# A spectral convolution block and a selective-scan block on one core: the first projection in two halves side by side, first transfers in order of need, the 64-channel block first, pieces of x asked for earlier

## The chip, the cores and the metric

The kernel runs on one core of a Trainium2 chip, in one launch. The metric is the device time of that core in microseconds (us). A core has five engines that run their own instruction streams in order and wait for each other by semaphores: PE (TensorE, matrix products into PSUM), DVE (VectorE), ACT (ScalarE), POOL (GpSimd) and SP (SyncE, which issues every DMA of this kernel). Sixteen DMA engines carry out the transfers.

## The reference

Two layers over x of 16 images, 64 x 64 pixels, 96 channels, each with a group normalisation before it and a residual sum. The first upsamples by 2 in frequency, applies a quadratic activation between two linear maps, and filters down again. The second is a Mamba-like block with four scan directions:

```python
def _L0_conv_ref(x, W1, b1, W2, b2, coef):
    xu = _upsample_rfft(xc)
    h = h @ W1.T + b1
    h = coef[:, 0] + coef[:, 1] * h + coef[:, 2] * (h * h)
    h = h @ W2.T + b2
    hl = _lpf_rfft(hc, cutoff=0.5)
    out = hl[:, :, ::2, ::2]
...
def _L1_conv_ref(x):
    xz = jnp.einsum('bhwc,pc->bhwp', x, in_proj_w)
    xc, z = (xz[..., :d], xz[..., d:])              # d = 192
    z = silu(z)
    xc = silu(depthwise_3x3(xc) + conv_b)
    xs = jnp.stack([x0, x1, x0[..., ::-1], x1[..., ::-1]], axis=1)   # rows, columns, both reversed
    x_dbl = jnp.einsum('bkdl,kcd->bkcl', xs, x_proj_weight)
    dts, Bs, Cs = jnp.split(x_dbl, [R, R + N], axis=2)               # R = 6, N = 16
    dts = jnp.einsum('bkrl,kdr->bkdl', dts, dt_projs_weight)
    # delta = softplus(dts + bias); h = exp(delta * A) * h + delta * u * B; y = sum_n h * C
    ys = selective_scan(xs, dts, As, Bs, Cs, Ds, dt_projs_bias)
    # y: the four directions summed, layer norm, times z
    return jnp.einsum('bhwd,cd->bhwc', y, out_proj_w)
...
x = x + _L0_conv_ref(_gn(x))
x = x + _L1_conv_ref(_gn(x))
```

## The kernel before

The program is written out engine by engine in its final order (`tc.manual_schedule()`); nothing reorders it. Its parts are generators, and a `yield` in them is the end of a slice.

**front(mi)** (L240) makes everything of an image that the scan needs. It normalises the image and goes over 100 rows of the upsampled picture in four passes of 25 (L313). A pass fetches x in three pieces of 32 channels, `fetch_x(cg)` (L264), four DMAs of 128 KB and two buffers each, multiplies them with the upsampling matrix (`u_ps`, L324) and copies the result to `t1` (L335). Then come five groups of five rows: `xu` (widened and normed), `h_ps` (L365), squares `hsq` on ACT (L348), `o_ps` (L377). Each second group is narrowed again and stowed in DRAM (`narrow`, `stow`, L303). Pieces of x, xu, hsq and others share eleven buffers (`piece`, L192). In each pass the first piece is asked for at the pass's start (L316), followed by three empty slices; the next one after the products of the one before (L331).

The second half of front computes the depthwise convolution as nine products with shifted pictures (L482), silu on ACT, and the z branch. It runs over two blocks of channels, `for i, n, tiles, both` (L461): first the 128 channels in eight tiles, then the 64 others in four tiles with two halves of the picture side by side. `turn` (L466) copies each tile into `col`, the column-wise order (L467), and stores rows and z in DRAM (L473, L474). After a block `col` is stored: for the 128 channels as four DMAs of 512 KB (L508, the helper's L199), for the 64 channels as eight DMAs of 128 KB in runs of 32 elements, 128 bytes (L513). `col` has one buffer, tag b16; the convolution's picture `xgp` and t1 have one other, tag b18.

**project(mi, pair, lc, out)** (L633) makes delta, delta * u, B and C of one step: a stretch of T = 1024 positions, in two halves of TB = 512 one after the other (L651). For a half it loads u in three parts (L645), multiplies them with the projection (`pp`, L655), adds the bias (`pr`, L659), and for each third of the channels, in the order 0, 2, 1: `s` (L666); softplus on ACT by way of |s|, exp, relu, ln (e, m, w, d: L674 to L681); four products with the identity that add up w, e, d, m (L686); dtu on DVE (L691), delta copied on ACT (L692); both stored in DRAM (L695, L696). B and C go to `rows` (L669). Every tile of it has one buffer.

**scan()** (L615) runs 128 steps (16 images, two pairs of directions, four stretches) of 24 units, 3072 in all. A unit covers 128 rows of (channel, state) twice: `drive` b = dtu * B on POOL (L761); `decay` exp(delta * A) on ACT (L755); the recurrence on DVE (L770, L772); the product with C on POOL (L917), DVE (L927), or DVE at every fifth unit (L909); the read-out on PE (L794). b, c, dtu and delta are loaded from DRAM with repetition (L703, L722). Decay runs one unit ahead, drive two.

Beside the units runs the background. Three times in a unit `slot` (L852) takes a slice of the next step's projection and one of the next image's front; when front is through, of the last image's finish. `Background` (L822) paces them: SLICES = 550 weights of front and finish over POS = 576 slots of an image.

Before the scan nothing runs beside anything: front of image 0, the whole first projection (L738), then the loads of eight b and c, of dtu and of delta (L740 to L742), then `drive` for two units and `decay` for one (L866 to L869). After it comes finish of the last image.

Of the kernel before, what the change touches and what calls it, by code (L numbers as in the profile page):

```python
# [45 lines left out]
F32 = mybir.dt.float32  # L46
# [25 lines left out]
SLICES = 550  # L72
# [7 lines left out]
def tile_two_blocks(  # L80
# [159 lines left out]
    def front(mi):  # L240
# [71 lines left out]
        o_last = None  # L312
        for p0 in range(0, UPS, PP):  # L313

            t1 = b18.tile([HW, PP, C], F32, name="t1", tag="b18")
            xr = fetch_x(0)  # L316
            for _ in range(3):
                yield
            for cg in range(3):
                u_ps = [bank([HW, 16, PP], "u_ps") for _ in range(2)]  # L320
                for k in range(16):
                    for a in range(2):
                        on = slice(64 * a, 64 * a + 64)
                        nc.tensor.matmul(  # L324
                            u_ps[a][:, k, :], lhsT=xr[k // 8][on, k % 8, :], rhs=up_s[on, p0:p0 + PP],
                            start=True, stop=True,
                        )
# [13 lines left out]
            for g in range(PP // PG):  # L341
# [119 lines left out]
        for i, n, tiles, both in ((0, 128, 8, 0), (1, 64, 4, 4)):  # L461
# [153 lines left out]
    def scan():  # L615


        with ExitStack() as es:
# [9 lines left out]
            banks.append(es.enter_context(tc.tile_pool(name="b_ps", bufs=2, space=PSUM)))  # L628
            aps = es.enter_context(tc.tile_pool(name="sc_aps", bufs=2, space=PSUM))
            yps = es.enter_context(tc.tile_pool(name="sc_yps", bufs=1, space=PSUM))  # L630
            gps = es.enter_context(tc.tile_pool(name="sc_gps", bufs=1, space=PSUM))

            def project(mi, pair, lc, out):  # L633
# [3 lines left out]
                out["rows"] = rows = dctx.tile([2, 2 * NS, T], F32, name="rows")  # L637
                out["delta"] = [dctx.tile([128, T], F32, name=f"delta_d{v}") for v in range(3)]
                out["dtu"] = [dctx.tile([128, T], F32, name=f"dtu_d{v}") for v in range(3)]
                xs_d = image[mi]["xs"]  # L640
                order = (0, 2, 1)

                def fetch_u(v, t):
                    uv = up_.tile([128, TB], F32, name="u")
                    nc.sync.dma_start(out=uv, in_=xs_d[v, :, lc * T + t:lc * T + t + TB])  # L645
                    return uv

                ahead_u = [fetch_u(v, 0) for v in order]
                for _ in range(4):
                    yield  # L650
                for t in range(0, T, TB):  # L651
                    u, ahead_u = dict(zip(order, ahead_u)), []
                    pp = gps.tile([128, TB], F32, name="pp", tag="g")
# [4 lines left out]
                    pr = pj.tile([128, TB], F32, name="pr")  # L658
# [3 lines left out]
                    for i, v in enumerate(order):  # L662
                        if i == 0:
                            yield
                        s = gps.tile([128, TB], F32, name="s", tag="g")
# [7 lines left out]
                        e, d, m, w = (pj.tile([128, TB], F32, name=k) for k in ("e", "d", "m", "w"))  # L673
# [9 lines left out]
                        s = gps.tile([128, TB], F32, name="s", tag="g")  # L683
# [5 lines left out]
                        dtu = pj.tile([128, TB], F32, name="dtu")  # L689
                        delta = pj.tile([128, TB], F32, name="delta")  # L690
# [6 lines left out]
                        if t + TB < T and i < 2:  # L697
# [364 lines left out]
```

## Time and profile before

| | us |
|---|---|
| median of 3 runs | 21647.74 (21629.93 to 21659.27) |
| profiled execution | 21651.91 |
| its span, first to last instruction | 21650.1 |
| first tile of the convolution starts on PE | 320.29 |
| first projection starts on PE | 438.13 |
| first product of the scan on POOL | 538.28 |
| first scan on DVE | 542.99 |
| last image's finish, from | 21497 |

The profiled execution and its span lie 1.8 us apart. In the profile a line such as "538.28 8.95 POOL L761 ..." of a timeline reads: start, duration, engine, line of the kernel, operation, output <- inputs with their shapes, how often, and in brackets how long the engine was idle before it and what ended that. SPq lines are DMA issues on SP. A line of the waits reads: what waited <- for what: us in total, times, longest. The granted TensorE clock was 0.857 in the mean.

### The profile page before, as it was taken

The page shows a single profiled execution, that of the slowest core. Times are in us where ns is not written, and L with a number is a line of the kernel's source. Part 1 is how long each engine was busy: PE and PEld are TensorE (multiplying, and loading weights), DVE is VectorE, ACT ScalarE, POOL GpSimd, SP SyncE. Part 2 cuts the span into 40 slices and gives each one's busy share as a digit, 9 for nine tenths or more (in the row PEclk, how much of TensorE's full clock was granted, in tenths as well). Part 3 has the DMA queues.
Part 4 walks back from the last instruction along what each step waited for, and adds up shares of the span by engine and source line. Part 5 has one row for each costly group of instructions (what it writes and reads, how often), then busy time and mean ns, then how long its engine had stood idle before and what let it go on. Part 6 is the DMA issues. An engine that isn't in the chain of part 4 may idle for free. (4 is left out here: it accounts for less than half of the span.)

```text
span 21650.1 us, 273738 instructions
## 1 busy us (share of the span) xinstructions
PE 16910.3 (78%) x98988; PEld 7341.1 (34%) x98988; DVE 19532.7 (90%) x12983; ACT 13726.8 (63%) x20546; POOL 19514.3 (90%) x5538
## 2 busy tenths in 40 slices
PE   7776877877778787887778788787787778877855
PEld 4423324233342333324333242333423333243221
DVE  0999999999999999999999999999999999999997
ACT  3666666666666666666666666676666666666553
POOL 0999999999999999999999999999999999999996
PEclk8887888988889888888888888888898888988977
DMA  2565565656656566565655656566565665656654
GB/s 71 182 206 183 201 220 185 222 188 204 217 184 224 185 216 200 191 226 180 219 194 201 221 183 215 192 204 213 191 226 182 214 201 193 225 181 219 216 188 141
DMA packets 1855467, 4277.13 MB, mean 198 GB/s; under 512 B 449438, under 2 KB 548670, under 8 KB 1852062
## 3 DMA queue, kind: packets, MB, share of 16 engines
q1 hardware_dynamic: 1854110, 4259.62, 59.0%
q8 instruction: 781, 12.80, 0.3%
q14 instruction: 576, 4.72, 0.1%
HBM read 3380.58 MB, written 878.18 MB: 197 GB/s over the span
## 5 line engine op out<-in xcount | busy, mean ns | idle before, releaser
L761 POOL TENSOR_TENSOR b<-dtu,bt 128x2048 f32<-128x2048 f32 x3072 | 13898.6, 4531 | 1341.2 <-PE y L794 617.3
L755 ACT ACTIVATE da<-delta,a_s 128x1024 f32<-128x1024 f32 x6144 | 6845.6, 1116 | 3099.3 <-DVE b L770 795.3
L917 POOL TENSOR_TENSOR b<-b,ct 128x1024 f32<-128x1024 f32 x2458 | 5798.8, 2359 | 631.1 <-DVE new L778 291.2
L794 PE MATMUL y<-b,fold_s 128*32 128x256 f32 x49152 | 3623.5, 420 | 331.3 <-DVE b L927 141.1
L927 DVE TENSOR_TENSOR b<-da,ct 128x1024 f32<-128x1024 f32 x3072 | 3756.6, 1223 | 93.9
L770 DVE TENSOR_TENSOR_SCAN da<-da,new,b 128x1024 f32<-128x1024 f32 x1383 | 3247.0, 2348 | 386.8 <-ACT da L755 361.7
L772 DVE TENSOR_TENSOR_SCAN da<-da,new,b 128x1024 f32<-128x1024 f32 x1382 | 3242.8, 2346 | 230.3 <-ACT da L755 212.4
L794 PEld LDWEIGHTS y<-b,fold_s 128*32 128x32 f32 x49152 | 1386.6, 117 | 2917.1 <-issue 1271.0
L686 PE MATMUL s<-w,ident_s 128*128 128x512 f32 x1536 | 1212.9, 882 | 1345.3 <-ACT w L681 1265.6
L772 DVE TENSOR_TENSOR_SCAN b<-da,new,b 128x1024 f32<-128x1024 f32 x922 | 2157.9, 2340 | 45.9 <-ACT da L755 36.3
L770 DVE TENSOR_TENSOR_SCAN b<-da,new,b 128x1024 f32<-128x1024 f32 x921 | 2156.3, 2341 | 13.3 <-ACT da L755 8.5
L778 ACT COPY new<-da 128x1 f32<-128x1 f32 x2764 | 434.6, 157 | 2723.5 <-DVE b L927 2195.3
L482 PE MATMUL c_ps<-xgp,wtap_s 96*128 96x512 f32 (+1 forms) x4608 | 1694.3, 635 | 163.2 <-ACT row L500 158.7
L666 PE MATMUL s<-pr,dtw_s 128*128 128x512 f32 x1536 | 1005.9, 741 | 1000.2 <-ACT pr L659 495.9
L365 PE MATMUL h_ps<-xu,w1t_s 96*128 96x500 f32 x1920 | 1044.0, 644 | 293.7 <-ACT hsq L348 120.6
L377 PE MATMUL o_ps<-w2c_s,hsq 128*100 128x96 f32 x9600 | 1061.3, 270 | 187.0 <-ACT hsq L348 161.8
L772 DVE TENSOR_TENSOR_SCAN da<-da,b 128x1024 f32<-128x1024 f32 x461 | 1055.9, 2291 | 120.4 <-ACT da L755 120.0
L770 DVE TENSOR_TENSOR_SCAN da<-da,b 128x1024 f32<-128x1024 f32 x460 | 1053.7, 2291 | 121.0 <-ACT da L755 116.5
L655 PE MATMUL pp<-u,xpt_s 128*128 128x512 f32 x1536 | 922.1, 741 | 305.7 <-DMA u<-xs_d 205.0
L377 PEld LDWEIGHTS o_ps<-w2c_s,hsq 128*100 128x100 f32 x9600 | 992.2, 182 | 393.0 <-ACT hsq L348 218.9
L686 PE MATMUL s<-e,ident_s 128*128 128x512 f32 x1536 | 1088.3, 800 | 0.0
L482 PEld LDWEIGHTS c_ps<-xgp,wtap_s 96*128 96x128 f32 (+1 forms) x4608 | 611.5, 173 | 1113.8 <-issue 896.3
(128 smaller groups left out, 21643.8 us busy)
## 6 DMA issues: line engine op xcount, KB each, us to landing
dtu<-dtu_d SPq DMA_DIRECT2D x1536, 512.0 KB
delta<-delta_d SPq DMA_DIRECT2D x1536, 512.0 KB
bt<-rows SPq DMA_DIRECT2D x1024, 512.0 KB
ct<-rows SPq DMA_DIRECT2D x1024, 512.0 KB
u<-xs_d SPq DMA_DIRECT2D x896, 256.0 KB
dtu_d<-dtu SPq DMA_DIRECT2D x768, 256.0 KB
delta_d<-delta SPq DMA_DIRECT2D x768, 256.0 KB
xr<-in_x SPq DMA_DIRECT2D x768, 128.0 KB
```

Source lines behind the costliest of these rows:

```text
L365: nc.tensor.matmul(h_ps[j], lhsT=w1t_s[:, 128 * j:128 * (j + 1)], rhs=xu.rearrange("c p q -> c (p q)"), start=True, stop=True,)
L377: nc.tensor.matmul(o_ps[:, p, :], lhsT=hsq[j][:, UPS * p:UPS * (p + 1)], rhs=w2c_s[:, j, :], start=(j == 0), stop=(j == HB - 1),)
L482: nc.tensor.matmul(c_ps[p:p + n], lhsT=wtap_s[:, tap, 128 * i:128 * i + n], rhs=xgp[:, h0:h0 + 8, dx:dx + HW], start=(tap == 0), stop=(tap ...
L666: nc.tensor.matmul(s, lhsT=dtw_s[:, pair, v, :], rhs=pr, start=True, stop=True)
L686: nc.tensor.matmul(s, lhsT=ident_s, rhs=of, start=(k == 0), stop=(k == 3))
L755: nc.scalar.activation(da, deltas[n // NQ, e], AF.Exp, scale=a_s[:, k, g, units[n][2]:units[n][2] + 1])
L761: nc.gpsimd.tensor_mul(b, dtus[n // NQ], bt.unsqueeze(1).to_broadcast([128, 2, T]))
L770: nc.vector.tensor_tensor_scan(out, da, b, before, ALU.mult, ALU.add)
L772: nc.vector.tensor_tensor_scan(out[:, ::-1], da[:, ::-1], b[:, ::-1], before, ALU.mult, ALU.add)
L794: nc.tensor.matmul(y[32 * q:32 * q + 32, e, :], lhsT=fold_s, rhs=b[:, e, QT * q:QT * q + QT], start=(pair == 0 and j == 0 and e == 0), sto ...
L917: nc.gpsimd.tensor_mul(h, h, bc[1, r, j])
L927: nc.vector.tensor_mul(bs[n][:, 0, :], h, bc[1, r, j])
```

## The change

Five edits. The first step's projection is started as two generators, one for each half, that take turns slice by slice; the second has buffers of its own, cut out of the b16 and b18 buffers (`far_u`, `far_w`), and both share four PSUM banks (`side_ps`), so the scan's PSUM pools are opened after it. As soon as one third of the channels is stored for both halves, the first b, dtu and delta are asked for; the seven other loads of b and c follow the projection. In front the 64-channel block comes before the 128-channel one. Pieces of x are kept in a list: the first pass asks for two at its start and for the third after the first products; in each pass's last group of rows the first two pieces of the next pass are asked for. The three empty slices thus remain in the first pass only, and SLICES goes from 550 to 541. For all later steps project runs as before, both halves in one generator.

```diff
-SLICES = 550
+SLICES = 541
...
         o_last = None
+        asked = []
         for p0 in range(0, UPS, PP):
 
             t1 = b18.tile([HW, PP, C], F32, name="t1", tag="b18")
-            xr = fetch_x(0)
-            for _ in range(3):
-                yield
+            if not asked:
+                asked += [fetch_x(0), fetch_x(1)]
+                for _ in range(3):
+                    yield
             for cg in range(3):
+                xr = asked.pop(0)
...
-                if cg < 2:
-                    xr = fetch_x(cg + 1)
+                if cg == 0:
+                    asked.append(fetch_x(2))
                 yield
...
                     if j == 2 and sd is not None:
                         stow(sd, row - 2 * PG)
+                    if j >= 2 and g == PP // PG - 1 and p0 + PP < UPS:
+                        asked.append(fetch_x(j - 2))
...
-        for i, n, tiles, both in ((0, 128, 8, 0), (1, 64, 4, 4)):
+        for i, n, tiles, both in ((1, 64, 4, 4), (0, 128, 8, 0)):
...
-            banks.append(es.enter_context(tc.tile_pool(name="b_ps", bufs=2, space=PSUM)))
-            aps = es.enter_context(tc.tile_pool(name="sc_aps", bufs=2, space=PSUM))
-            yps = es.enter_context(tc.tile_pool(name="sc_yps", bufs=1, space=PSUM))
-            gps = es.enter_context(tc.tile_pool(name="sc_gps", bufs=1, space=PSUM))
-
-            def project(mi, pair, lc, out):
+            def project(mi, pair, lc, out, ps, half=None, own=None):
...
+                halves = range(0, T, TB) if half is None else (half,)
+
+                def make(name):
+                    return own(name) if own else pj.tile([128, TB], F32, name=name)
...
-                ahead_u = [fetch_u(v, 0) for v in order]
+                ahead_u = [fetch_u(v, halves[0]) for v in order]
...
-                for t in range(0, T, TB):
+                for t in halves:
...
-                        if t + TB < T and i < 2:
+                        out["made"] += 1
+                        if half is None and t + TB < T and i < 2:
...
-            for _ in project(*steps[0], ctxs[0]):
-                pass
-            bc = {(what, 0, j): fetch_bc(ctxs[0], 0, j, what) for j in range(NQ) for what in range(2)}
-            dtus = {0: fetch_dtu(ctxs[0], 0)}
-            deltas = {(0, e): fetch_delta(ctxs[0], 0, e) for e in (1, 0)}
+
+            bc, dtus, deltas = {}, {}, {}
+
+            far_u = b16.tile([128, 4, TB], F32, name="far_u", tag="b16")
+            far_w = b18.tile([128, 6, TB], F32, name="far_w", tag="b18")
+            far = {f"u{v}": far_u[:, v, :] for v in range(3)}
+            far["pr"] = far_u[:, 3, :]
+            far.update({k: far_w[:, i, :] for i, k in enumerate(("e", "d", "m", "w", "dtu", "delta"))})
+            with tc.tile_pool(name="side_ps", bufs=4, space=PSUM) as side:
+                todo = [project(*steps[0], ctxs[0], side, 0), project(*steps[0], ctxs[0], side, TB, far.get)]
+                while todo:
+                    todo = [g for g in todo if next(g, todo) is not todo]
+                    if ctxs[0]["made"] >= 2 and not dtus:
+                        bc[0, 0, 0] = fetch_bc(ctxs[0], 0, 0, 0)
+                        dtus[0] = fetch_dtu(ctxs[0], 0)
+                        for e in (1, 0):
+                            deltas[0, e] = fetch_delta(ctxs[0], 0, e)
+            for j in range(NQ):
+                for what in range(2):
+                    if (what, 0, j) not in bc:
+                        bc[what, 0, j] = fetch_bc(ctxs[0], 0, j, what)
+            banks.append(es.enter_context(tc.tile_pool(name="b_ps", bufs=2, space=PSUM)))
+            aps = es.enter_context(tc.tile_pool(name="sc_aps", bufs=2, space=PSUM))
+            yps = es.enter_context(tc.tile_pool(name="sc_yps", bufs=1, space=PSUM))
+            gps = es.enter_context(tc.tile_pool(name="sc_gps", bufs=1, space=PSUM))
+
...
-                    step_gen = Background(project(*steps[st], ctxs[st]), PSLICES, 3 * per_step)
+                    step_gen = Background(project(*steps[st], ctxs[st], gps), PSLICES, 3 * per_step)
```

More of the change, by code (lines that the diff above doesn't have):

```diff
@@ L627, in scan @@
             dctx = es.enter_context(tc.tile_pool(name="dctx", bufs=3, space=bass.MemoryType.DRAM))
-            banks.append(es.enter_context(tc.tile_pool(name="b_ps", bufs=2, space=PSUM)))
-            aps = es.enter_context(tc.tile_pool(name="sc_aps", bufs=2, space=PSUM))
-            yps = es.enter_context(tc.tile_pool(name="sc_yps", bufs=1, space=PSUM))
-            gps = es.enter_context(tc.tile_pool(name="sc_gps", bufs=1, space=PSUM))
-            def project(mi, pair, lc, out):
-                out["rows"] = rows = dctx.tile([2, 2 * NS, T], F32, name="rows")
-                out["delta"] = [dctx.tile([128, T], F32, name=f"delta_d{v}") for v in range(3)]
-                out["dtu"] = [dctx.tile([128, T], F32, name=f"dtu_d{v}") for v in range(3)]
+            def project(mi, pair, lc, out, ps, half=None, own=None):
+                if not out:
+                    out["rows"] = dctx.tile([2, 2 * NS, T], F32, name="rows")
+                    out["delta"] = [dctx.tile([128, T], F32, name=f"delta_d{v}") for v in range(3)]
+                    out["dtu"] = [dctx.tile([128, T], F32, name=f"dtu_d{v}") for v in range(3)]
+                    out["made"] = 0
+                rows = out["rows"]
                 xs_d = image[mi]["xs"]
                 order = (0, 2, 1)
+                halves = range(0, T, TB) if half is None else (half,)
+                def make(name):
+                    return own(name) if own else pj.tile([128, TB], F32, name=name)
                 def fetch_u(v, t):
-                    uv = up_.tile([128, TB], F32, name="u")
+                    uv = own(f"u{v}") if own else up_.tile([128, TB], F32, name="u")
                     nc.sync.dma_start(out=uv, in_=xs_d[v, :, lc * T + t:lc * T + t + TB])
                     return uv
-                ahead_u = [fetch_u(v, 0) for v in order]
+                ahead_u = [fetch_u(v, halves[0]) for v in order]
                 for _ in range(4):
                     yield
-                for t in range(0, T, TB):
+                for t in halves:
                     u, ahead_u = dict(zip(order, ahead_u)), []
-                    pp = gps.tile([128, TB], F32, name="pp", tag="g")
+                    pp = ps.tile([128, TB], F32, name="pp", tag="g")
                     for v in range(3):
@@ L657, in project @@
                         yield
-                    pr = pj.tile([128, TB], F32, name="pr")
+                    pr = make("pr")
                     nc.scalar.activation(pr, pp, AF.Identity, bias=bumps_s)
@@ L664, in project @@
                             yield
-                        s = gps.tile([128, TB], F32, name="s", tag="g")
+                        s = ps.tile([128, TB], F32, name="s", tag="g")
                         nc.tensor.matmul(s, lhsT=dtw_s[:, pair, v, :], rhs=pr, start=True, stop=True)
@@ L672, in project @@
                         yield
-                        e, d, m, w = (pj.tile([128, TB], F32, name=k) for k in ("e", "d", "m", "w"))
+                        e, d, m, w = (make(k) for k in ("e", "d", "m", "w"))
                         nc.scalar.activation(e, s, AF.Abs)
@@ L682, in project @@
                         yield
-                        s = gps.tile([128, TB], F32, name="s", tag="g")
+                        s = ps.tile([128, TB], F32, name="s", tag="g")
                         yield
@@ L688, in project @@
                             yield
-                        dtu = pj.tile([128, TB], F32, name="dtu")
-                        delta = pj.tile([128, TB], F32, name="delta")
+                        dtu, delta = make("dtu"), make("delta")
                         nc.vector.tensor_mul(dtu, s, u[v])
```

## The prediction

> **What bounds the kernel now.** I read the page's busy shares first, then POOL's and DVE's timelines, then every engine's timeline from 390 to 546 us, then the waits.
>
> ```profile
> PE 16910.3 (78%) x98988; PEld 7341.1 (34%) x98988; DVE 19532.7 (90%) x12983; ACT 13726.8 (63%) x20546; POOL 19514.3 (90%) x5538
> DVE  0999999999999999999999999999999999999997
> POOL 0999999999999999999999999999999999999996
> ```
>
> DVE and POOL are full except in the first and last slice. The run is a start of 543 us in which they do nothing, a scan, and 153 us of end from 21497. The scan is 20954 us for 3072 units, 6.82 each, where POOL needs 4531 + 0.8 x 2359 ns = 6.42.
>
> ```profile
> 538.28 8.95 POOL L761 TENSOR_TENSOR b<-dtu,bt 128x2048 f32<-128x2048 f32 x2 [537.27 <-DMA dtu<-dtu_d]
> 547.19 2.35 POOL L917 TENSOR_TENSOR b<-b,ct 128x1024 f32<-128x1024 f32 x1
> ```
>
> POOL's first work waits for a load until 538.28. Whatever shortens the start is worth itself, as long as the scan is fed. What stands ahead of it:
>
> ```profile
> 427.91 1.05 ACT L467 COPY col<-row 128x512 f32<-128x512 f32 x1
> 428.98 5.76 SPq L513 DMA_DIRECT2D xs_d<-col  x8
> 438.13 5.46 PE L655 MATMUL pp<-u,xpt_s 128*128 128x512 f32 x6 [12.18 <-DMA u<-xs_d]
> ...
> 461.00 0.71 ACT L681 ACTIVATE w<-w,one_s 128x512 f32<-128x512 f32 x1
> 461.77 2.08 PE L686 MATMUL s<-w,ident_s 128*128 128x512 f32 x2 [3.66 <-ACT w L681]
> 466.96 0.69 DVE L691 TENSOR_TENSOR dtu<-s,u 128x512 f32<-128x512 f32 x1 [10.65 <-PE s L686]
> ...
> 520.99 0.58 ACT L692 COPY delta<-s 128x512 f32<-128x512 f32 x1 [7.26 <-DVE dtu L691]
> 521.97 0.56 SPq L722 DMA_DIRECT2D bt<-rows  x1
> 540.73 2.15 ACT L755 ACTIVATE da<-delta,a_s 128x1024 f32<-128x1024 f32 x2 [19.16 <-DMA delta<-delta_d]
> 542.99 2.29 DVE L770 TENSOR_TENSOR_SCAN b<-da,b 128x1024 f32<-128x1024 f32 x1 [22.03 <-ACT da L755]
> ```
>
> The last column copy, the stores of its result, two projection halves one after the other (438 to 521), then twelve loads, and only then the first unit. In the projection ACT and PE take turns: ACT makes e, m, w, d in 3.6 us, PE's eight passes with the identity take 5.2 to 6.3, DVE and ACT drain in 1.3. Neither engine is full.
>
> ```profile
> 150.55 0.41 PE L324 MATMUL u_ps<-up_s,xr 64*64 64x25 f32 x2 [4.92 <-DMA xr<-in_x]
> PE u_ps L324 <- DMA xr<-in_x: 74.2, 49, 4.3
> POOL b L761 <- PE y L794: 617.3, 365, 8.3
> DVE da L770 <- ACT da L755: 478.3, 421, 3.4
> ```
>
> PE waits for pieces of x: 4.92 us at the third pass of the start, and 49 times (74.2 us) under the scan, about one wait of 4 us an image. The last two lines show how such a delay gets to the full engines: through PE's read-out, which frees b for POOL, and through ACT's decay, which DVE's scan reads.
>
> **What the Trainium skill says.** "TensorE: Matmul & The Clock Gate", Part 1 (the HAM clock gate): the array runs at half rate until about 3.4 us of sustained work have passed, and falls back when idle. The trace agrees: identity passes follow each other every 0.85 us after an idle stretch (451.08, 451.94, 452.79) and every 0.43 after a longer run (465.04, 465.47, 465.90). The same part calls ACT and DVE strict FIFO; so the order written into the program is the order in which the two halves run. "DMA: Bandwidth & Descriptors", Specifications: below 512 B per piece a transfer loses line rate. The eight stores of 128 B pieces moved mostly 160 to 200 GB/s, the four whole ones of the other block 380 to 437. The same page, "Anatomy of one DMA — SWDGE (gpsimd) path", gives about 2 us fixed to a transfer, for GpSimd's path; on SP's path here 2.96 us lie between the issue at 147.59 and the use at 150.55.
>
> **The change part by part.** Times are of the profiled execution: span 21650.1, 21651.9 with what lies around it; the median of the runs is 21647.7.
>
> *Order of the two blocks.* A tile of either block takes 8.58 us (rows on ACT at 382.05 and 390.64, 399.38 and 407.97), so the last copy still ends at 428.96. Behind it, four whole stores take 2.87 us to issue (394.53) in place of 5.76, but u's third load needs the first of them, and the second half's loads go into the column's buffer and wait for all four, some 6 us. First pp at about 436.6: 1.5 us saved (0 to 3).
>
> *Two halves side by side.* Nothing is removed; the same instructions interleave A, B, A, B on each engine. A round for one third of the channels: draining B 1.35 us on DVE and ACT; then twelve ACT operations, of which A's are ready after ten, 5.9; A's eight passes, cold at first, 6.0; B's eight behind them, warm, 8 x 0.43 = 3.4; gaps 0.4. That is 17 us for two, against 11.3 to 13.0 for one; 17.5 taken. If PE stays cold it is 20.4, if A warms up early 16. The first round: pp for A 5.1 from 436.6, pp for B 2.7, s 1.2, ACT to 451.6, passes to 461.5, drain to 463. With two rounds more (35) and a margin of 2 the last copy ends at 500 instead of 521.57. Of these 21.5 us, 1.5 are the order's, 20 this edit's. Bounds: 14 and 25.
>
> *First transfers in order of need.* Before, 16.7 us pass from the last copy to POOL's first product and 21.4 to the first scan. Now the first bt, dtu and delta (five loads, 2.6 MB) are issued after the first third of both halves, near 465, and land by 477 at the 370 GB/s of the first loading (mean of 521 to 545), while PE and ACT project. POOL's first product (4.5 us) runs under the projection; decays follow the last copy at once: first scan near 502.5, 40.5 earlier. But the second product needs the second bt, which still comes after everything, behind one ct: about 506, so POOL has both products at 511 instead of 547.2. POOL sets the pace there (it ran on without a gap to 592), so 36 of the 40.5 count: 14.5 by this edit. The remaining loads, 512 KB each in 1.3 us, arrive faster than the 6.8 us of a unit. If the second bt is late or SP is held by the last stores, 3 to 6 us less.
>
> *Pieces of x further ahead, in the start.* The loads now stand on SP before the stow of the narrowed rows that held them. The six waits of passes two to four (4.92, 0.34, 0.21, 0.19, 0.16, 0.16) go: 5.5. The first pass has norm as cover either way.
>
> Start: 1.5 + 20 + 14.5 + 5.5 = 41.5 us. The end is untouched.
>
> *Under the scan, fifteen images.* Three empty slices go from three of four passes, so front has 380 slices instead of 389, and with SLICES 541 the end of the background stays where it was (two or three slots of 576 differ). Every piece of work moves by up to nine slots. Three effects. First, PE's waits for x (up to 4 us an image) go; POOL shows idle time of 1 to 2 us after about half of them: 0 to 1.5 us an image. Second, SP's order: before, four groups of x loads an image stand within five transfers ahead of a block's second delta load, the one with least time in hand; after, two, one of them by a single load. Near 854 us such a group was followed by 2.9 us of ACT waiting for delta. But of 143 such waits only 19 (49 us) have x loads in the 6 us before them, with 27 us of DVE idle near them: 0 to 1 us an image. Third, against it: the next pass's products come with no free slots before them, two groups are asked in adjacent slices, a megabyte at once, and the two convolution blocks change places; behind PE wait the read-outs, behind ACT the decays. The trace can't show this new arrangement. Images of the same program take 1279 to 1320 us, so I allow from 3 us less to 2.5 us more an image (-45 to +37) and take 12 us less in all.
>
> Sum: 41.5 + 12 = 53.5; 21651.9 - 53.5 = 21598.4. The median lies 4 below the profiled run; between the two, 21597.
>
> **Rivals.**
> *The start is won, and the scan gives it back.* One or two us an image lost by the shifted background, through the two waits shown above. For: DVE's and POOL's idle time (1232 us of waits summed over the timeline, and 20954 - 19514 = 1440) comes from where PE and ACT happen to be. Against: no work is added. 21652 - 41.5 + 25 = 21635.
> *The halves don't overlap.* In-order engines and a cold PE could make a round cost two single ones. For: PE idles over 3.4 us in each round. Against: ACT and PE are free for half of each chain now. Start gains 21.5 only: with the scan's 12, 21618.
> *The scan improves strongly.* If both effects of x loads count whole and the smoother front lets ACT's decays through: 4 us an image beyond the start, 21652 - 41.5 - 60 = 21550.
> *Slower.* One mechanism: x loads fetched two groups at once put 1 MB, 2.7 us at 370 GB/s and 5 us of issue on SP, in front of delta and dtu loads, three times an image; ACT's decays, then DVE wait. It decides once it costs over (41.5 + 43) / 15 = 5.6 us an image; at 8 us an image: 21652 - 41.5 + 120 = 21730. Against: the order of issue shows fewer x loads right ahead of delta.
>
> **How the numbers follow.** This measurement tells 0.2%, 43 us, from no change. Forecast (35 to 75 us won) 0.50, of which 0.44 lies beyond 43 us; strong scan 0.15; given back 0.20; no overlap 0.06; slower 0.09. Faster 0.59, same 0.32, slower 0.09. The range, 21540 to 21650, takes in the unknown of the scan on both sides and leaves out the slower case and the far end of the strong one.
>
> **What would show it.** After, with the 5.5 us of the passes taken off too: the last projection copy near 494.5 (488 to 501), first scan near 497, POOL's second product ended near 505.5, no wait for xr above 1 us in the start, and from the first scan to the first product of the end (20954 us before) some 20940, within 45. Wrong if the copies end after 505 (overlap), if the first scan waits over 5 us for ct or bt, or if the scan itself is longer than 20990.

## The result and the profile after

After the change the kernel takes 21570.46 us (median of 7 runs, 21554.29 to 21582.71) against 21647.74 (7 runs, 21629.93 to 21672.05) before: 0.9956 of it, 95% interval 0.9947 to 0.9965. The two medians lie 77 us apart, a ratio of 0.9964, which is within the interval. The two profiled executions lie 97.6 us apart (21554.29 and 21651.91), mostly because the profiled one of after is the lowest of its seven, 16 us below their median. Every split below is made on the profiled executions and so adds up to some 20 us more than the medians show.

The page's busy shares and its 40 slices for DVE and POOL, after:

```profile
PE 16756.6 (78%) x98988; PEld 7278.2 (34%) x98988; DVE 19473.3 (90%) x12983; ACT 13728.1 (64%) x20546; POOL 19513.6 (91%) x5538
DVE  0899999999999999999999999999999999999997
POOL 0899999999999999999999999999999999999996
```

Both engines are as full as before. POOL's work is the same to 0.7 us, so 97.6 us can only have come from stretches in which it idled. One thing differs: DVE is busy 59 us less with the same 12983 instructions.

The timeline of after around the end of the projection (start, duration, engine, line, operation):

```profile
431.15 4.98 PE L663 MATMUL pp<-u,xpt_s 128*128 128x512 f32 x6 [11.65 <-DMA u<-xs_d]
463.85 4.51 POOL L790 TENSOR_TENSOR b<-dtu,bt 128x2048 f32<-128x2048 f32 x1 [462.84 <-DMA dtu<-dtu_d]
467.33 3.60 PE L694 MATMUL s<-far_w,ident_s 128*128 128x512 f32 x8
488.54 0.58 ACT L699 COPY far_w<-s 128x512 f32<-128x512 f32 x1 [2.85 <-DVE far_w L698]
489.15 2.15 ACT L784 ACTIVATE da<-delta,a_s 128x1024 f32<-128x1024 f32 x2
491.80 2.29 DVE L799 TENSOR_TENSOR_SCAN b<-da,b 128x1024 f32<-128x1024 f32 x1 [3.29 <-ACT da L784]
495.96 4.50 POOL L790 TENSOR_TENSOR b<-dtu,bt 128x2048 f32<-128x2048 f32 x1 [27.60 <-DMA bt<-rows]
500.42 2.34 POOL L946 TENSOR_TENSOR b<-b,ct 128x1024 f32<-128x1024 f32 x1
```

POOL's first product now runs under the projection (463.85). The decay follows the last copy at once (488.54, 489.15) and the first scan starts at 491.80, before at 542.99: 51.2 us earlier. POOL's second product, which waits for the second bt, ends at 500.46, before at 547.23: 46.8 us earlier. From the first scan to the last one it was 20941.7 us before (542.99 to 21484.68) and is 20891.3 (491.80 to 21383.07): 50.4 less. The end, from the last scan on, went from 165.4 to 169.4. So 51.2 + 50.4 - 4.0 = 97.6. The start came out close to its sum, while the scan gave four times what was put down for it. (On the medians the scan's part would be about 30 us: an estimate, 77.3 - 51.2 + 4.0, that takes the start and the end as the profiles have them.)

Where the scan's part shows, in the groups of DVE by line (busy us, mean ns of one, idle before), first of before, then of after:

```profile
L236 DVE TENSOR_TENSOR nb<-nmean,rg 96x1 f32<-96x1 f32 x32 | 160.8, 5025 | 331.0 <-ACT rg L233 330.8
```

```profile
L236 DVE TENSOR_TENSOR nb<-nmean,rg 96x1 f32<-96x1 f32 x32 | 90.4, 2824 | 312.6 <-ACT rg L233 312.6
```

`nb` is the product of two columns of 96 numbers, made once in each of the two norms of an image. Alone, in the start, it takes 0.15 us. In the scan it held DVE for 5.3 us each time, now for 3.0; the means in the rows, 5025 and 2824 ns, count the two of the start too. The change doesn't touch it. The prediction had not looked at this row.

### The profile page after: what moved, and what is told of

Read it like the earlier page. It is cut to its first block, busy times and chain, and to the rows that moved or that the text cites. A ratio compares the mean times of both kernels' runs of the same rounds, so it can differ in the third digit from the quotient of the medians.

```text
span 21552.5 us, 273639 instructions
## 1 busy us (share of the span) xinstructions
PE 16756.6 (78%) x98988; PEld 7278.2 (34%) x98988; DVE 19473.3 (90%) x12983; ACT 13728.1 (64%) x20546; POOL 19513.6 (91%) x5538
## 5 line engine op out<-in xcount | busy, mean ns | idle before, releaser
L694 PE MATMUL s<-w,ident_s 128*128 128x512 f32 x1530 | 1150.5, 843 | 1278.1 <-ACT w L689 1262.7
L487 PE MATMUL c_ps<-xgp,wtap_s 96*64 96x512 f32 (+1 forms) x4608 | 1707.2, 634 | 252.2 <-ACT row L505 246.6
L370 PE MATMUL h_ps<-xu,w1t_s 96*128 96x500 f32 x1920 | 1110.4, 680 | 430.0 <-ACT xu L285 166.6
L694 PE MATMUL s<-e,ident_s 128*128 128x512 f32 x1530 | 1019.2, 756 | 0.0
L487 PEld LDWEIGHTS c_ps<-xgp,wtap_s 96*64 96x64 f32 (+1 forms) x4608 | 600.3, 170 | 1197.4 <-issue 891.3
```

The lines of the kernel that those rows point to most:

```text
L370: nc.tensor.matmul(h_ps[j], lhsT=w1t_s[:, 128 * j:128 * (j + 1)], rhs=xu.rearrange("c p q -> c (p q)"), start=True, stop=True,)
L487: nc.tensor.matmul(c_ps[p:p + n], lhsT=wtap_s[:, tap, 128 * i:128 * i + n], rhs=xgp[:, h0:h0 + 8, dx:dx + HW], start=(tap == 0), stop=(tap ...
L694: nc.tensor.matmul(s, lhsT=ident_s, rhs=of, start=(k == 0), stop=(k == 3))
```

## The experiments

Each is a copy of one of the two kernels with one edit or one part of the change. Times are medians; each ratio is to the kernel before on the same chip (medians of before there: 21660.53, 21655.26, 21650.63 and 21655.24 for the four groups below).

### One part of the change at a time

**e1_start_only**: the two halves side by side and the first transfers in order of need alone.

```diff
-            for _ in project(*steps[0], ctxs[0]):
-                pass
+            todo = [project(*steps[0], ctxs[0], side, 0), project(*steps[0], ctxs[0], side, TB, far.get)]
...
```

> The kernel before with the first projection in two halves and the first transfers in order of need, nothing else. All theories: the first scan starts near 498 instead of 543 (the projection 25 us shorter, 19 us less from its last copy to the first scan), POOL's second product ends near 507 instead of 547. If the start alone is worth what it shows, the time falls by 40 us to about 21608. The scan keeps its length (20942 from first to last scan, within 15) in every theory: nothing of it is changed, and nb (L236 on DVE) stays near 161 us in all.

**e2_pieces_only**: the pieces of x as in after, with the empty slices dropped from passes two to four and SLICES 541; blocks and projection as before.

```diff
-SLICES = 550
+SLICES = 541
...
-            xr = fetch_x(0)
-            for _ in range(3):
-                yield
+            if not asked:
+                asked += [fetch_x(0), fetch_x(1)]
+                for _ in range(3):
+                    yield
...
+                    if j >= 2 and g == PP // PG - 1 and p0 + PP < UPS:
+                        asked.append(fetch_x(j - 2))
```

> The kernel before with the pieces of x asked for earlier and SLICES 541. Start: 11 us shorter. Theory NB (the scan's gain comes from DVE being held less long by nb, whose slot moved): nb falls from 161 to about 90 us, for both norms stand in the same slots as in the changed kernel, and the scan loses 35 us or more; time 21600. Theory X (the gain comes from x loads that no longer stand before delta loads): the same time, with ACT's waits for delta down from 373 to about 210 us. This run alone does not part the two; the next ones do.

**e3_order_only**: the 64-channel block first, nothing else.

```diff
-        for i, n, tiles, both in ((0, 128, 8, 0), (1, 64, 4, 4)):
+        for i, n, tiles, both in ((1, 64, 4, 4), (0, 128, 8, 0)):
```

> The kernel before with the 64-channel block first and nothing else. Theories NB and X: the scan stays within 15 us, the start gets 3.5 us longer (the first convolution tile waits for more of the normed picture), time within 15 us of before. Theory ORDER (the block order is what eased the scan): the scan is 30 to 50 us shorter, time 21605.

**e4_slices_only**: the number of slices alone, so that the background moves while none of its work changes.

```diff
-SLICES = 550
+SLICES = 541
```

> The kernel before with SLICES 541 instead of 550, nothing else: pieces of x are asked for as before. The first norm's nb moves from slot 0 to slot 1 of a unit as in the changed kernel, the second norm's from slot 2 to slot 1. Theory NB: nb falls to 80 to 110 us, the scan is 25 to 50 us shorter, time about 21610. Theory X: ACT's waits for delta stay near 373 us and the time stays at 21648 within 15. Theory ORDER: no change either.

| | median us | ratio, 95% interval | first scan | first to last scan | nb on DVE, us |
|---|---|---|---|---|---|
| before | | | 542.99 | 20941.7 | 160.8 |
| after | 21570.46 | 0.9956 [0.9947, 0.9965] | 491.80 | 20891.3 | 90.4 |
| e1 | 21612.21 | 0.9982 [0.9975, 0.9989] | 500.71 | 20943.4 | 150.6 |
| e2 | 21559.19 | 0.9956 [0.9944, 0.9969] | 530.37 | 20858.7 | 107.4 |
| e3 | 21582.25 | 0.9965 [0.9953, 0.9977] | 539.51 | 20863.4 | 153.4 |
| e4 | 21769.27 | 1.0050 [1.0038, 1.0063] | 542.53 | 21063.3 | 122.8 |

Of these four, e1 alone came near what was expected of it. e2 came out 41 us below the 21600 of both its theories. e3's scan is 78 us shorter, where theory ORDER had 30 to 50 and the two others nothing. e4 goes against all three: nb fell to 122.8 us, yet the scan grew by 122.

The edits don't add up: alone, they win 48, 101 and 78 us, which makes 227, and together 77. The start stands by itself (e1's scan is as long as that of before). Under the scan, e4 is the strongest of all and does no useful thing: the same work in other slots costs 109 us.

To see where, the scan was cut into bins of 12 units (192 units an image) and each bin averaged over images 1 to 14. Here are the eight bins that differ most, in us, worked out from the starts of DVE's scans. Within a bin the images spread by mostly 1 to 2 us (standard deviation; up to 4 in the bin at 84), so that a mean of 14 is good to about half a us, in the bin at 84 to one:

```
units     before   e1     e2     e3     e4    after   e8     e6     e9
  0- 11    85.9   85.8   85.4   85.8   84.5   85.2   85.5   82.4   85.9
 36- 47    84.2   84.3   80.9   84.0   84.6   80.8   81.0   84.2   82.6
 60- 71    78.4   78.3   83.1   78.5   80.1   83.2   82.9   78.2   83.7
 84- 95    83.5   82.8   80.9   82.6   82.0   80.1   81.5   77.2   84.2
 96-107    80.3   80.3   88.2   80.6   92.0   90.0   88.4   80.9   80.4
108-119    89.6   90.0   81.5   81.5   85.9   76.8   81.6   90.2   89.4
120-131    85.4   85.2   87.0   87.3   85.8   91.6   87.9   85.7   86.0
132-143    80.3   80.5   78.0   81.7   78.8   80.4   78.0   80.4   80.4
```

Read it by columns. e1 equals before to 0.7 in every bin. e3 equals before to 0.9 up to unit 107 and parts from it then, where the two blocks lie. In bins 0 to 95 after follows e2 to 0.8, since up to there the background is the same. So the cost of background work is local to the units it falls on, and repeats from image to image. In the convolution (84 to 143) the sum is 419.1 before, 413.7 with e3, 415.6 with e2, 418.9 after, 424.5 with e4: the new block order wins in the old slots, and in after, with both edits, nothing is left of either gain there.

### The interaction, and the instruction that holds DVE

**e5_after_550**: after, with the old number of slices.

```diff
-SLICES = 541
+SLICES = 550
```

> The changed kernel with SLICES back at 550. The norms' nb goes back to slot 0 and slot 2 of a unit, as in the kernel before; x pieces, block order and start stay changed. Theory NB: nb rises from 90 to 140 to 160 us, the scan gets 25 to 50 us longer, time about 21605. Theory X and theory ORDER: as the changed kernel, 21570 within 12.

**e6_before_nb_act** and **e7_after_nb_act**: nb on ACT, in the kernel before and in the one after.

```diff
-        nc.vector.tensor_mul(nb, nmean, rg)
+        nc.scalar.activation(nb, nmean, AF.Identity, scale=rg)
```

> The kernel before with one instruction moved: nb = nmean * rg runs on ACT right behind rg, so that DVE no longer waits for ACT there. Theory NB: DVE wins 161 us of held time and up to 330 us of idle time before it; as POOL and ACT hold it back elsewhere, the scan is 60 to 130 us shorter, time about 21555. Theories X and ORDER: nb's time was slack that something else fills, the scan within 20 us, time 21648 within 20.

> The changed kernel with nb on ACT. Theory NB: what is left of nb (90 us held, part of the 313 us before it) goes, 40 to 90 us less than the changed kernel, about 21505, the fastest so far. Theories X and ORDER: 21570 within 12.

**e8_after_old_order**: after, with the 128-channel block first again.

```diff
-        for i, n, tiles, both in ((1, 64, 4, 4), (0, 128, 8, 0)):
+        for i, n, tiles, both in ((0, 128, 8, 0), (1, 64, 4, 4)):
```

> The changed kernel with the 128-channel block first again. Theories NB and X: start 3.5 us shorter, scan within 15 us, time 21567 within 15. Theory ORDER: the scan gets 30 to 50 us longer, time about 21610.

| | median us | ratio, 95% interval | first to last scan | nb on DVE, us |
|---|---|---|---|---|
| e5 | 21644.08 | 0.9995 [0.9987, 1.0004] | 20984.1 | 161.1 |
| e6 | 21545.36 | 0.9949 [0.9937, 0.9962] | 20832.1 | none |
| e7 | 21484.98 | 0.9921 [0.9908, 0.9935] | 20813.9 | none |
| e8 | 21533.79 | 0.9945 [0.9932, 0.9957] | 20874.8 | 103.1 |

With 550 slices the whole gain of the change is gone (e5). The rise of nb in e5 is what theory NB said, the loss is more than it said, and X and ORDER, which had no change, are refuted there. nb off DVE is worth 110 us before (e6) and some 80 after (e7: 86 between medians from two groups of runs, 76 by the ratios), close to what NB expected. In e6 the gain lies in the two bins that hold the norms, -3.5 us in 0 to 11 and -6.3 in 84 to 95; the other bins together give 2.6 back. e8 came out faster than after, which no theory had. Still it isn't the whole of the scan's difference: e4 has 38 us less of nb than before and a scan 122 us longer. (Its second norm falls in another bin: nb there takes 6.2 us an image in units 96 to 107, where before has none, so about half of e4's 11.7 us in that bin is nb in a new place.) The new block order, which wins 78 us by itself, costs 37 in after (21570.46 against e8's 21533.79, from two groups of runs; the intervals of 0.9956 and 0.9945 overlap, so the size is uncertain, while e3's gain is not).

### Loads, or slots?

**e9_early_loads**: the early loads of x alone; the empty slices and 550 stay.

```diff
-            xr = fetch_x(0)
+            if not asked:
+                asked += [fetch_x(0), fetch_x(1)]
             for _ in range(3):
                 yield
...
+                    if j >= 2 and g == PP // PG - 1 and p0 + PP < UPS:
+                        asked.append(fetch_x(j - 2))
```

> The kernel before with the pieces of x asked for early, but with the three empty slices of every pass and SLICES 550 kept, so that every slice stays in its slot. Theory LOADS (the early loads are what the pieces bring): PE's waits for x under the scan go from 74 us to under 5, ACT's waits for delta from 369 to about 240, the scan falls by most of the 83 us that the pieces with SLICES 541 brought, 50 or more, and in units 24 to 48 of an image by 6 us. Theory PLACE (the slot in which each slice lands is what counts): the same fewer waits, but the scan falls by less than 30 us, and units 84 to 192 of an image keep their times within 1 us per 12 units. Start 11 us shorter in both.

**e10_no_empty**: the other half of e2: no empty slices in passes two to four, 541, and the loads as late as before.

```diff
-SLICES = 550
+SLICES = 541
...
-            for _ in range(3):
+            for _ in range(0 if p0 else 3):
```

> The kernel before without the empty slices in passes two to four and with SLICES 541, the loads of x where they were, right before their use: every slice in the slot that it has with early pieces. Theory PLACE: the scan falls by half or more of the 83 us, and units 84 to 192 take the times of the run with early pieces, although PE's waits for x rise above 150 us. Theory LOADS: PE waits for x at every pass, the scan is 20 to 100 us longer than before.

**e11_old_order_nb_act**: after with the old block order and nb on ACT.

> The changed kernel with the 128-channel block first again and nb on ACT, the two edits that helped it one at a time (37 and 85 us). If what each slice costs stays local to its units, they add up: scan near 20800, first scan near 492, time 21455 within 15, the fastest. If they take the same waits away, no more than the better of the two: 21485.

e9 takes 21718.23 (1.0038 [1.0025, 1.0050]), e10 21577.47 (0.9964 [0.9950, 0.9978]), e11 21431.08 (0.9902 [0.9888, 0.9915]). PE's waits for x are gone in e9, where the kernel is slower, and longer in e10 (93.9 us, before 74.2), where it is faster. In units 84 to 191 every bin of e10 is within 0.8 us of e2, and every bin of e9 within 0.7 of before, as theory PLACE had it; PE's waits rose less than its 150. So it isn't the loads that win but the slots in which the work falls once three empty slices are gone. e11 is the fastest kernel of this study, 219.5 us below before, and 24 us below the 21455 that adding up its parts gave. That is outside the 15 us allowed, but far from the 21485 of parts that take the same waits away: with the number of slices kept, the costs add up roughly. (It is also 54 us below e7, from which it differs in the block order alone.)

e9 also shows what the loads do. The timeline of e9 at unit 60 of an image, then that of before at the same place:

```profile
7551.53 1.27 SPq L303 DMA_DIRECT2D s_d<-sd  x2
7552.90 5.05 SPq L270 DMA_DIRECT2D xr<-in_x  x8
...
7559.31 0.59 SPq L708 DMA_DIRECT2D delta<-delta_d  x1
...
7566.11 2.15 ACT L760 ACTIVATE da<-delta,a_s 128x1024 f32<-128x1024 f32 x2 [7.76 <-DMA delta<-delta_d]
7567.26 2.36 DVE L775 TENSOR_TENSOR_SCAN da<-da,new,b 128x1024 f32<-128x1024 f32 x1 [6.01 <-ACT da L760]
```

```profile
7513.95 1.28 SPq L303 DMA_DIRECT2D s_d<-sd  x2
...
7516.59 0.59 SPq L703 DMA_DIRECT2D delta<-delta_d  x1
...
7524.10 2.15 ACT L755 ACTIVATE da<-delta,a_s 128x1024 f32<-128x1024 f32 x2 [3.34 <-DMA delta<-delta_d]
7525.25 2.36 DVE L770 TENSOR_TENSOR_SCAN da<-da,new,b 128x1024 f32<-128x1024 f32 x1 [1.59 <-ACT da L755]
```

Eight issues of x (5.05 us of SP) stand between the store of the narrowed rows and the delta load. From store to delta's issue it is 7.78 us instead of 2.64; ACT waits 7.76 instead of 3.34, DVE 6.01 instead of 1.59. It happens once an image and costs 5.3 us of the bin at 60. An image of e9 is 6.7 us longer in its profile; the bin at 36 wins 1.6, and the remaining 3.0 are spread over the other bins. After pays it too: in the same image eight issues of x from 7442.72 on stand ahead of the delta load at 7451.23, ACT waits 6.01 us at 7462.77, and the bin stands at 83.2 against 78.4.

### What holds nb

Two things could hold a product of 96 numbers for 5 us: its input, which comes from ACT, or something that shuts DVE out. The timeline of before, of DVE, ACT and POOL at one nb:

```profile
5822.29 8.98 POOL L761 TENSOR_TENSOR b<-dtu,bt 128x2048 f32<-128x2048 f32 x2
5825.37 1.23 DVE L909 TENSOR_TENSOR b<-da,ct 128x1024 f32<-128x1024 f32 x1
5826.42 0.20 ACT L233 ACTIVATE rg<-var 96x1 f32<-96x1 f32 x1
5826.66 4.63 DVE L236 TENSOR_TENSOR nb<-nmean,rg 96x1 f32<-96x1 f32 x1
5831.22 2.28 DVE L770 TENSOR_TENSOR_SCAN da<-da,b 128x1024 f32<-128x1024 f32 x1
```

rg is there at 5826.62; nb starts then and ends at 5831.29, POOL's second product at 5831.27. Of the 30 nb under the scan, all end within 0.04 us of the end of a product on POOL, before and after alike. By the kernel's text nb and `lin` (L259, of the same stretch of front) are the only instructions of DVE under the scan that read two tensors in SBUF (the scans' start value `new` is a single column); scans, products with C and dtu have one operand in PSUM, where da and s lie. The copies `new`, with one input and that in SBUF, are not held in before:

```profile
L778 DVE COPY new<-b 128x1 f32<-128x1 f32 x1844 | 283.6, 154 | 63.1
```

1408 of the 1844 lie wholly within a product on POOL, and each of these takes 152 to 156 ns. The Trainium skill, "SBUF — State Buffer", section "Who interferes with whom", says just this: a DVE instruction with two SBUF inputs contends with a GpSimd instruction that reads SBUF; one with at most one SBUF input, outside the two-port modes, doesn't. **e12_nb_psum** keeps nb on DVE, at its place in the order, and moves one operand:

```diff
+        nc.scalar.activation(v_ps[:, 0:1], var, AF.Exp, scale=-0.5)
...
-        nc.vector.tensor_mul(nb, nmean, rg)
+        nc.vector.tensor_mul(nb, nmean, v_ps[:, 0:1])
```

> The kernel before, with one operand of nb changed: ACT writes rg a second time, into the PSUM tile v_ps, and DVE's product nb = nmean * rg reads it there. Engine, place and order of nb are kept; only one of its inputs now lies in SBUF instead of both. Theory LOCK: in the traces of before and after every one of the 30 nb under the scan ends within 0.04 us of the end of a POOL product, and DVE's other operations on that stretch have at most one input in SBUF; nb is shut out by POOL for as long as POOL's product runs. Then nb takes 0.15 to 0.3 us each (5 to 9 us in all instead of 160.8) and the kernel gains what e6_before_nb_act gained: ratio 0.993 to 0.997, median 21505 to 21575. Theory ACT (what the earlier experiments were read by): nb is held because its input comes late from ACT, or because it sits in DVE's order at all; then the records stay near 5 us (120 to 165 us in all), and with one ACT operation of 0.2 us more the time is 21640 to 21670, ratio 0.9995 to 1.001.

It takes 21541.34 us, 0.9947 [0.9933, 0.9960], the same as e6. The group of DVE, and one nb in the timeline, both of e12:

```profile
L237 DVE TENSOR_TENSOR nb<-nmean,v_ps 96x1 f32<-96x1 f32 x32 | 4.7, 147 | 329.8 <-ACT v_ps L234 329.5
```

```profile
5800.17 8.99 POOL L762 TENSOR_TENSOR b<-dtu,bt 128x2048 f32<-128x2048 f32 x2
5805.90 0.15 DVE L237 TENSOR_TENSOR nb<-nmean,v_ps 96x1 f32<-96x1 f32 x1
5805.97 2.29 DVE L771 TENSOR_TENSOR_SCAN da<-da,b 128x1024 f32<-128x1024 f32 x1
```

0.15 us in the middle of a POOL product, and 160.8 us have become 4.7. So POOL shuts nb out, as theory LOCK had it; ACT's rg, for which DVE still waits 330 us in all, costs nothing that shows. This also says why nb's cost changes with the slots: it depends on which POOL products are running when it falls due. The time of the 30 nb and the 15 lin under the scan, in us:

```
        before  after   e4     e5     e6    e7    e8     e9    e10    e11
nb      160.5   90.1  122.5  160.8    -     -   102.8  161.9  109.1    -
lin       3.7   22.1   16.8    3.7  25.5  10.2   26.4    3.7   21.7  10.3
```

With 550 slices and nb left as it was, both together make 154 to 166 (e1 154, e3 157); after has 112.2. The 52 us less are as large as the scan's gain of 50.4, but e4 shows that other slot costs of that size exist, so this isn't the sum of it.

## Why the prediction was right, and where it was not

The direction was right, and the sum of the start nearly so. The time is 27 us below the 21597 forecast, and the 77 us won lie just beyond the 35 to 75 of its likeliest case. Most of the excess is in the scan, and there the size came from something else than the causes named: that the sum still came near is in part luck. By its steps, on the profiled executions:

| step | predicted | measured |
|---|---|---|
| order of the blocks, in the start | -1.5 | +3.4 (first tile to last copy 108.7 to 112.6, last copy to first pp 9.17 to 8.65) |
| two halves side by side | -20 | first pp to last copy 83.4 to 58.0: -25.4 |
| first transfers | -14.5 | last copy to POOL's second product 25.7 to 11.3: -14.4 |
| pieces of x, in the start | -5.5 | -11.7 (first norm to second, 280.4 to 268.8): 10.7 of PE's busy time, 1.0 of its idle time |
| first norm, which starts the pieces' stretch | | +1.3 |
| sum, to POOL's second product | -41.5 | -46.8 |
| scan | -12 (-45 to +37) | -50.4 |
| end | 0 | +4.0 |

*Two halves.* The working held: the first round took 24.5 us where 26.4 were put down, the two others 16.6 and 16.9 where 17.5 each were, B's eight warm passes 3.60 where 3.4 were. The margin of 2 us wasn't needed. One reading was too neat: PE's half rate was taken to last about 3.4 us, and in before the passes stay 0.85 us apart for 3.3 us in the second third (461.77 to 465.04) but for 5.3 in the first (449.21 to 454.49). The range put down for a round covered this. The rival in which the halves don't overlap falls.

*First transfers.* As worked out, including the catch: the first scan starts 18.7 us sooner after the last copy, but POOL waits 27.60 us for its second bt, so less of it counts.

*Pieces, in the start.* The step was that the waits of passes two to four go. They didn't: they became other waits. PE's waits for x from 85 to 300 us, of before and then of after:

```profile
PE u_ps L324 <- DMA xr<-in_x: 6.0, 6, 4.9
PE u_ps L327 <- DMA xr<-in_x: 5.5, 5, 1.7
```

One wait of 4.92 us has made room for three of 1.60 to 1.74, so the sign "no wait for xr above 1 us in the start" failed. What shortened the stretch is PE's busy time: for the same 1878 products it went from 240.92 to 230.24 us, at a higher granted clock. The windows of the second and third pass, before and then after (us, busy of PE, PEld, DVE, ACT, POOL, granted clock, DMA share, GB/s):

```profile
90.00:150.00 60.00, 53.13 (x435) 38.39 (x434) 0.00 (x0) 21.62 (x35) 0.00 (x0) 0.78 0.15 37
150.00:205.00 55.00, 52.05 (x429) 39.06 (x430) 0.00 (x0) 19.94 (x32) 0.00 (x0) 0.75 0.16 41
```

```profile
91.00:143.00 52.00, 47.93 (x437) 34.89 (x436) 0.00 (x0) 20.54 (x34) 0.00 (x0) 0.84 0.19 56
143.00:195.00 52.00, 48.07 (x457) 33.88 (x457) 0.00 (x0) 21.58 (x35) 0.00 (x0) 0.87 0.14 36
```

About the same number of products takes PE 48 us at a clock of 0.84 to 0.87 instead of 52 to 53 at 0.75 to 0.78. How much of this follows from the early loads, the other runs tell only in part. The stretch from norm to norm takes 275.8 to 284.9 us in the seven profiles with late loads (mean 279.5) and 268.4 to 277.5 in the seven with early ones (271.3), with the same products in all. PE idles 39.2 to 41.3 us of it with late loads and 36.7 to 38.5 with early ones. So the early loads are worth some 3 us of idle time and about 5 of faster products in the mean; why the products run faster is not shown, and a single pair of profiles can be off by several us.

*Order.* The sign was wrong. The prediction gave a tile of either block 8.58 us, so that the last copy would end where it did. But the first tile of the 64-channel block needs both halves of the picture, which ACT is still norming. The timeline of before, then of after:

```profile
320.29 10.21 PE L482 MATMUL c_ps<-xgp,wtap_s 96*128 96x512 f32 x18 [4.51 <-ACT xgp L454]
330.54 0.69 ACT L500 ACTIVATE row<-c_ps,convb_s 128x512 f32<-128x512 f32 x1 [4.07 <-PE c_ps L482]
```

```profile
309.90 1.97 PE L487 MATMUL c_ps<-xgp,wtap_s 96*64 96x512 f32 x2 [4.51 <-ACT xgp L459]
312.72 10.85 PE L487 MATMUL c_ps<-xgp,wtap_s 96*64 96x512 f32 x33 [0.85 <-ACT xgp L459]
324.03 0.69 ACT L505 ACTIVATE row<-c_ps,convb_s 128x512 f32<-128x512 f32 x1 [7.95 <-PE c_ps L487]
```

From the first product to the first row it is 14.1 us instead of 10.3. PE waits again for the picture, and its weight loads stand 0.85 us apart until 8.9 us after the first product, in before until 3.6. From first tile to last copy the four profiles with this order take 111.5 to 112.6 us, the ten others 108.3 to 109.3; the shorter way from copy to pp gives 0.6 back in the mean. So the edit costs the start about 3 us. (e3's first scan comes 3.5 us sooner than that of before only because its stretch between the norms, where the order is not yet at work, took 275.8 us instead of 280.4.)

*Scan.* This is the step that failed most. The prediction gave 12 us to two causes: PE's waits for x, and fewer x loads ahead of delta. The first is there but small: e9 removes those waits, and of the eight bins only that at 36 gets clearly shorter, by 1.6 us an image, while the kernel is 68 us slower. The second is refuted as told. ACT's waits for delta under the scan did fall, from 350 to 207 us, but they fall to 161 in e10, which has no early load, and rise to 382 in e9, which has them; and in after eight loads stand ahead of a delta at unit 60, as in e9, and the bin is 4.8 us longer than before. That is the mechanism of the slower rival, and it was real, but it strikes once an image rather than three times and costs 5.3 us there in e9, short of the 5.6 from which it would have decided. What won was treated only as a risk, under "Every piece of work moves by up to nine slots": with 541 slices and the empty ones gone, work falls into other units (e10, without any early load, wins 73 us), and the norms fall where nb is held little more than half as long. How much of the 50.4 us each slot gives stays open. The strong-scan rival had the size (3.4 us an image against its 4) for a cause that doesn't hold. The row of nb, 5025 ns for 96 numbers, stood in the groups by line of before; reading that view by mean duration against size would have shown 160 us of a full engine gone, and that its size hangs on the slot.

*Open:* why each of the convolution's slots costs what it does; in e4's bin at 96, 5.5 of the 11.7 us are not nb. e4's granted clock is also lower in all five runs, 0.851 to 0.853 against 0.854 to 0.859, and whether that is cause or effect is not shown. e3 and e8 show that block order and slots interact there; no run isolates the wait.

## What to carry to other kernels

Background work that is dealt out in slots to in-order engines has a price by slot, so edits to it don't add up: measure each alone and both together, and compare unit by unit, where the mean over many images shows a difference of 1 us. On a kernel that fills both DVE and POOL, look in the groups for small instructions with a long mean, and keep one operand of such a product on DVE in PSUM, or the instruction on ACT: each was worth about 110 us here (e12, e6). Before moving a load earlier, count what it puts ahead of the load with the least time in hand.

## What the hardware showed that was not expected

The DVE product that POOL shuts out often doesn't get in at the next boundary between two POOL products: 17 of the 30 in before pass over at least one, two of them over three. The timeline of before, the longest nb:

```profile
16947.50 4.51 POOL L761 TENSOR_TENSOR b<-dtu,bt 128x2048 f32<-128x2048 f32 x1
16951.10 12.15 DVE L236 TENSOR_TENSOR nb<-nmean,rg 96x1 f32<-96x1 f32 x1
16951.98 2.35 POOL L917 TENSOR_TENSOR b<-b,ct 128x1024 f32<-128x1024 f32 x1
16954.30 8.94 POOL L761 TENSOR_TENSOR b<-dtu,bt 128x2048 f32<-128x2048 f32 x2
```

It waits out four products that follow each other, 12.15 us, and ends with the last, after which POOL has nothing to do. In before, POOL idles 2.35 to 9.91 us after 29 of the 30, 147 us in all. Likely its next work needs what DVE could not make meanwhile, so that a tiny product stops first one full engine, then the other; e12, which takes the hold away, wins 114 us.
